# Second pointwise layer and guides as seven block products in 28 of 32 blocks of a fused attention and perception kernel

## The chip, the cores and the metric

The kernel runs on one core of a Trainium2 chip. The metric is device time of one execution in microseconds (us), as a median over runs. The engines are TensorE (PE; its weight loads are shown as PEld), VectorE (DVE), ScalarE (ACT), GpSimd (POOL) and SyncE (SP, which issues most DMAs). Each engine works through its own instructions in the order in which the program issued them. Everything is float32.

## The reference

Two layers over images of 4 x 64 x 64 pixels with 256 channels:

```python
# layer 0: global attention, per image, over its 4096 pixels
q = x @ Wq + bq;  k = x @ Wk + bk            # 32 channels each
v = x @ Wv + bv                              # 256 channels
x = gamma * (softmax(q @ k.T) @ v) + x
# layer 1: perception and 3x3 local attention
perceived = depthwise_conv3x3(x, w_perc) + b_perc        # 256 -> 768 channels
hid = gelu(w_up1 @ perceived + b_up1)                    # 768 -> 512
h   = x + w_up2 @ hid + b_up2                            # 512 -> 256, "second pointwise layer"
q, k, v = split(w_qkv @ h + b_qkv)                       # 256 each
out = h + sum over the 3x3 neighbours n of softmax_n(q . k[n] / 16) * v[n]
```

## The kernel before

**Slots.** The work is cut into 32 slots (`NSLOT`), one for each block of 512 query pixels (8 image rows); 8 slots make an image. In slot `s` PE computes the global attention of block `s`, while the later stages of earlier blocks run beside it: the depthwise convolution (`perceive`) of block `s - 2`, then for block `k = s - 3` the first pointwise layer (`hidden_part`), the second (`update`), guides (`guide`), the scores and the values of the local attention, and for block `a = s - 5` the local attention's output (`local_product`).

**Points.** A slot has 16 points, one for each 256 keys. The order is written out by hand: at each point the program issues, in this order, the energies and exponentials of a later point, the *jobs* of the point (the list `jobs`, L943), the attention's product (eight matmuls in the trace, L313), DVE's softmax add `add_up` (L327), and a share of the convolution's steps (taps on DVE, L468, and sums of quarters, L474; 60 steps over 14 points). Every engine receives its instructions in this order, so a DVE instruction of a job stands behind the taps of the point before.

**Block products.** A pointwise layer is a matrix product. `hidden_part` already writes it by blocks: the weight and the values are cut 2 x 2, and seven products of blocks with half the rows and half the columns take the place of eight, at the price of sums and differences of blocks. The differences of weights (`wmix`, from `mix_weights`, on POOL) are made once; those of values are made for each block on DVE (L474, then L539 on the results).

**The second layer and guides, before.** `update(s, c)` (L584) multiplies for each of two channel halves four weight blocks of 128 x 128 by 512 pixels of `hid` into one PSUM bank. DVE adds the bias and `x` and writes `h` in two column halves (L595). After the second half `border_terms` (L714) puts the image edge's terms into `edge` (DVE, L718 and L719). `guide(s, i)` (L667) does the same with `wg`, the product of the local query and key weights, and ACT writes the result with its bias into `guides` (tile `lq`, L681). In the job list the updates stand at points 6 and 7, point 8 has no job, and guides stand at 9 and 10, before the scores at 11 and 12.

**PSUM.** Jobs take their banks in turn from two (`job_bank`), so a job's matmuls wait until the results of the job two before have been read.

**Last slot and tail.** Slot 31 has a job list of its own. After it, blocks 29 to 31 are finished in a written order (`run`, L1047), in which DVE's last taps (`conv`) are dealt out between the jobs. `local_total` (L857) is PE's sum for the local softmax, `border` (L730) its edge term. `local_product` (L871) multiplies by the inverse sum on DVE (L889) and adds `h`: on POOL (L899) for most blocks, on DVE for blocks 28, 29 and 31. POOL also adds everything it is shown to `watched` (`watch`, L186), whose sum decides at the end whether a slower second path has to run (it does not here).

Of the kernel before, what the change touches and what calls it, by code (L numbers as in the profile page):

```python
# [15 lines left out]
P = 128  # L16
# [36 lines left out]
def attention_then_perception_kernel(  # L53
# [34 lines left out]
    def unshifted():  # L88
# [132 lines left out]
        def project_qk(s):  # L221

            ps = bank("m", f"qk_{s}")
            for kin in range(CH):
                for r in range(2):
                    nc.tensor.matmul(  # L226
                        ps[2 * r * CQK : 2 * (r + 1) * CQK, :],
                        lhsT=wqk[:, kin].rearrange("p s d -> p (s d)"),
                        rhs=staged[s + r][:, kin, :], start=(kin == 0), stop=(kin == CH - 1),
                    )  # L230
            st = tile_of([P, NB], "st", f"st_{s}")
            nc.scalar.activation(st, ps, AF.Identity, bias=bqk2)
            if s == 0:
                queries[0] = tile_of([P, NB], "qa", "qa_0", 2)
                for j in range(GRP):
                    nc.sync.dma_start(
                        out=queries[0][j * CQK : (j + 1) * CQK, :], in_=st[:CQK, :]
                    )
            for r in range(2):
                at = 2 * r * CQK  # L240
                keys[s + r] = tile_of([P, P], "ka", f"ka_{s + r}", NBLK + 1)
                queue = nc.sync if s + r else nc.scalar
                for j in range(GRP):
                    queue.dma_start(
                        out=keys[s + r][j * CQK : (j + 1) * CQK, :],
                        in_=st[at + CQK : at + 2 * CQK, bass.ts(j, P)],
                    )
                if s + r:
                    nc.sync.dma_start(
                        out=packed[:, bass.ts(s + r, NB)], in_=st[at : at + CQK, :]  # L250
                    )

        def project_v(s, pair, tag="m"):
            xc = staged[s]
            if pair == 0:
                values[s] = tile_of([P, TPB, C], "v", f"v_{s}", NBLK + 1)
# [173 lines left out]
            return thirds.pop(0)  # L430

        def spare(name):
            return tile_of([P, TPB, C], "v", name, NBLK + 1).rearrange(
                "p (a t) c -> p a (t c)", a=2
            )

# [68 lines left out]

        wmix = pool.tile([P, 4, MULT, C], F32, tag="wmix", name="wmix")

        def mix_weights():
            y = [[wup1[:, i * MULT : (i + 1) * MULT, bass.ts(j, C)] for j in range(2)] for i in range(2)]
            for to, a, b in (  # L510
                (0, y[0][1], y[0][0]), (1, y[1][1], wmix[:, 0]), (2, y[1][1], y[0][1]),
                (3, y[1][0], wmix[:, 1]),
            ):
                nc.gpsimd.tensor_tensor(wmix[:, to], a, b, ALU.subtract)

        def hidden_part(s, d, part):

# [66 lines left out]
        def update(s, c):  # L584
# [17 lines left out]
            if c == CH - 1:  # L602
                border_terms(s)

# [8 lines left out]
        def combine_steps():  # L613

            names, ws, turned = ("wq", "wk"), [], []
            ins, outs = (
                perc_tile(f"wqk_{name}").rearrange("p s n -> p (s n)") for name in ("in", "turned")
            )
            for i, name in enumerate(names):
                w = ins[:, i * NB : (i + 1) * NB].rearrange("p (k c) -> p k c", c=C)  # L620
                nc.sync.dma_start(out=w, in_=w_qkv[:, :, i * C : (i + 1) * C])
                ws.append(w)
            yield
            for i, (name, w) in enumerate(zip(names, ws)):
# [20 lines left out]
            nc.vector.tensor_copy(wg, ps.rearrange("p (k c) -> p k c", c=C))  # L645
            yield
# [20 lines left out]
        def guide(s, i):  # L667


            if s == 0 and i == 0:  # L670
                guides.append(tile_of([P, CH, UP + RB, W], "lq", "lq"))
                nc.vector.memset(guides[0][:, :, :UP, :], 0.0)
            elif i == 0:
                nc.scalar.copy(guides[0][:, :, :UP, :], guides[0][:, :, RB:, :])
            ps = job_bank(f"g_{s}_{i}")
            for kin in range(CH):
                nc.tensor.matmul(  # L677
                    ps, lhsT=wg[:, kin, bass.ts(i, P)], rhs=pixels(s, kin),
                    start=(kin == 0), stop=(kin == CH - 1),
                )  # L680
            nc.scalar.activation(  # L681
                guides[0][:, i, UP:, :].rearrange("p h w -> p (h w)"), ps, AF.Identity,
                bias=bg[:, i : i + 1],
            )


# [184 lines left out]
        def local_product(s, c, behind=None):  # L871
# [18 lines left out]
            if s < NSLOT - 1:  # L890
                watch(o)
            engine, res = nc.gpsimd, o
            if s >= DIRECT and s != NSLOT - 2:

                if c == 0:
                    results[s] = tile_of([P, CH, NB], "xc", f"res_{s}", 2)
# [40 lines left out]
        for slot in range(NSLOT):  # L937
            b, g = divmod(slot, NBLK)
            if slot >= RING:
# [4 lines left out]
                job(hidden_part, k, 0, 0) + job(local_values, k - 1, 1),  # L944
                job(local_denominator, a) + job(hidden_part, k, 0, 1),
                job(hidden_part, k, 1, 0), job(hidden_part, k, 1, 1),
                job(local_product, a, 0), job(local_product, a, 1),
                job(update, k, 0), job(update, k, 1), [],
                job(guide, k, 0), job(guide, k, 1), job(scores, k, 0),
                job(scores, k, 1) + job(local_sum, k - 1), job(local_values, k, 0), job(border, k), [],  # L950
            ]
            if slot in (1, 2):
# [9 lines left out]
            n_mixed = NPC * (TAPS - 1) + MULT * len(MIXED)  # L962
            n_steps, stepped = n_mixed, 0
            if slot == NSLOT - 1:


                jobs = [
# [17 lines left out]
            for point in range(points):  # L985
# [27 lines left out]
                if slot == 0 and point == NG:  # L1013
# [8 lines left out]
                    mix_weights()  # L1022
# [34 lines left out]
        for _ in perceive(last - 1, lower):  # L1057
# [443 lines left out]
```

## Time and profile before

| what | before |
|---|---|
| median of 3 runs | 3495.58 us (3494.74 to 3495.85) |
| profiled execution: time | 3495.72 us |
| profiled execution: span | 3494.0 us |
| PE busy | 3473.1 us, 99% |
| DVE busy | 2493.2 us, 71% |
| ACT busy | 1084.0 us, 31% |
| POOL busy | 616.4 us, 18% |
| granted TensorE clock, mean | 0.998 |

A line of a timeline gives the start, the busy time, the engine, the source line and operation, output and inputs by name with their shapes, and how many instructions were merged; in brackets the idle time before it and who ended that. Spans of single instructions overlap where an engine pipelines them, so a step's cost is better read from one start to the next. Lines `L...` are those of the kernel before.

### The profile page before, as it was taken

The page shows a single profiled execution, that of the slowest core. Times are in us where ns is not written, and L with a number is a line of the kernel's source. Part 1 is how long each engine was busy: PE and PEld are TensorE (multiplying, and loading weights), DVE is VectorE, ACT ScalarE, POOL GpSimd, SP SyncE. Part 2 cuts the span into 40 slices and gives each one's busy share as a digit, 9 for nine tenths or more (in the row PEclk, how much of TensorE's full clock was granted, in tenths as well). Part 3 has the DMA queues.
Part 4 walks back from the last instruction along what each step waited for, and adds up shares of the span by engine and source line. Part 5 has one row for each costly group of instructions (what it writes and reads, how often), then busy time and mean ns, then how long its engine had stood idle before and what let it go on. Part 6 is the DMA issues. An engine that isn't in the chain of part 4 may idle for free.

```text
span 3494.0 us, 32246 instructions
## 1 busy us (share of the span) xinstructions
PE 3473.1 (99%) x12222; PEld 1907.4 (55%) x12222; DVE 2493.2 (71%) x3631; ACT 1084.0 (31%) x1330; POOL 616.4 (18%) x823
## 2 busy tenths in 40 slices
PE   9999999999999999999999999999999999999997
PEld 5444555555555555565555555556555555555655
DVE  2387777657777877765777777776577777777885
ACT  3233332333233233332332323333333323223331
POOL 2000112111121211121112212111121121121224
PEclk9999999999999999999999999999999999999999
DMA  4000000120000000011000000001100000000000
GB/s 105 7 4 10 7 16 11 27 48 22 9 12 11 16 16 16 22 25 46 16 16 16 3 13 16 16 22 37 34 16 16 16 9 10 13 16 16 7 6 26
DMA packets 92995, 66.82 MB, mean 19 GB/s; under 512 B 65856, under 2 KB 70976, under 8 KB 92704
## 3 DMA queue, kind: packets, MB, share of 16 engines
q1 hardware_dynamic: 92160, 64.29, 6.9%
q8 instruction: 98, 1.61, 0.2%
q14 instruction: 65, 0.53, 0.0%
q10 hardware_dynamic: 672, 0.39, 0.0%
HBM read 43.49 MB, written 18.81 MB: 18 GB/s over the span
## 4 chain that ended last, share of the span: by engine, by line
PE 98%; DVE 1%; POOL 1%; SPq 0%; DMA 0%; ACT 0%; issue 0%; ACTq 0%; POOLq 0%
PE acc L313 51%; PE e L294 8%; PE dx L589 6%; PE hid_de L532 4%; PE hid_gf L532 4%; PE hid_bc L532 4%; PE g L677 3%; PE lv L746 3%; PE v L260 3%; PE lo L877 3%; PE hid_a L532 3%; PE s L787 2%; PE hid L564 1%; PE qk L226 1%; DVE perc L468 0%; POOL watched L186 0%
## 5 line engine op out<-in xcount | busy, mean ns | idle before, releaser
L313 PE MATMUL acc<-p,v 128*128 128x512 f32 x4096 | 1841.5, 594 | 0.2 <-DVE o L378 0.2
L313 PEld LDWEIGHTS acc<-p,v 128*128 128x128 f32 x4096 | 765.9, 190 | 863.4 <-issue 854.4
L468 DVE SCALAR_TENSOR_TENSOR perc<-xp,wperc,perc 128x512 f32<-128x512 f32 (+2 forms) x1554 | 1157.6, 804 | 31.8 <-ACT perc L464 31.8
L302 ACT ACTIVATE p<-e 128x1024 f32<-128x1024 f32 x512 | 524.3, 1024 | 1673.9 <-PE e L294 617.7
L327 DVE TENSOR_TENSOR den<-den,p 128x1024 f32<-128x1024 f32 x480 | 586.0, 1221 | 99.2 <-ACT p L302 97.5
L186 POOL TENSOR_TENSOR watched<-watched,lo 128x256 f32<-128x256 f32 x124 | 150.8, 1216 | 1013.5 <-DVE lo L889 1008.5
L294 PE MATMUL e<-qa,ka 32*128 32x512 f32 x2048 | 291.9, 640 | 0.0
L811 POOL TENSOR_TENSOR lp<-lp,near 128x396 f32<-128x396 f32 x60 | 87.1, 1452 | 1123.8 <-ACT lp L807 1123.8
L589 PE MATMUL dx<-hid,wup 128*128 128x512 f32 x512 | 233.0, 598 | 0.0
L759 DVE TENSOR_TENSOR lv<-lv,blv 128x256 f32<-128x256 f32 x126 | 47.5, 419 | 210.4 <-PE lv L746 210.2
L474 DVE TENSOR_TENSOR perc<-perc 128x256 f32<-128x256 f32 x360 | 173.2, 495 | 7.2
L294 PEld LDWEIGHTS e<-qa,ka 32*128 32x128 f32 x2048 | 80.0, 182 | 166.2 <-issue 164.2
L589 PEld LDWEIGHTS dx<-hid,wup 128*128 128x128 f32 x512 | 94.6, 190 | 129.9 <-issue 101.7
L532 PE MATMUL hid_de<-perc,wmix 128*128 128x256 f32 x720 | 165.2, 379 | 0.0
L532 PEld LDWEIGHTS hid_de<-perc,wmix 128*128 128x128 f32 x720 | 136.8, 190 | 43.7 <-issue 21.5
L555 ACT ACTIVATE hid<-hid,bup 128x512 f32<-128x512 f32 x120 | 80.1, 715 | 214.3 <-DVE hid L539 214.3
L539 DVE TENSOR_TENSOR hid<-hid_bc,hid 128x512 f32<-128x512 f32 x60 | 41.5, 691 | 147.3 <-PE hid_bc L532 147.3
L464 ACT ACTIVATE perc<-xp,bperc,wperc 128x512 f32<-128x512 f32 x192 | 145.1, 805 | 0.0
L595 DVE SCALAR_TENSOR_TENSOR h<-dx,bup,xp 128x256 f32<-128x256 f32 x128 | 56.0, 479 | 116.2 <-PE dx L589 116.2
L677 PE MATMUL g<-h,wg 128*128 128x512 f32 x256 | 123.4, 605 | 0.2
L746 PE MATMUL lv<-wlv,h 128*128 128x256 f32 x520 | 122.4, 379 | 0.0
L877 PEld LDWEIGHTS lo<-lp,lv 128*128 128x128 f32 x732 | 102.9, 191 | 35.1 <-issue 27.0
(147 smaller groups left out, 2898.7 us busy)
## 6 DMA issues: line engine op xcount, KB each, us to landing
xp<-in_x SPq DMA_DIRECT2D x30, 528.0 KB, 4.0
out<-lo SPq DMA_DIRECT2D x58, 256.0 KB, 2.0
xc<-in_x SPq DMA_DIRECT2D x56, 256.0 KB, 3.8
qa<-packed SPq DMA_DIRECT2D x124, 64.0 KB, 2.1
ka<-st SPq DMA_DIRECT2D x124, 16.0 KB, 1.8
packed<-st SPq DMA_DIRECT2D x31, 64.0 KB, 1.9
wup<-in_w_up SPq DMA_DIRECT2D x1, 1536.0 KB, 6.9
out<-res SPq DMA_DIRECT2D x6, 256.0 KB, 2.2
```

The costliest lines, as they stand in the source:

```text
L186: nc.gpsimd.tensor_tensor(at, at, values[:, i : min(n, i + C)], ALU.add)
L294: nc.tensor.matmul(e[:, j, :], lhsT=key[rows, :], rhs=queries[s][rows, :], start=True, stop=True,)
L302: nc.scalar.activation(p, energies[s, G][:, 2 * half : 2 * half + 2, :], AF.Exp)
L313: nc.tensor.matmul(accs[s][c], lhsT=v[:, 2 * half + i, bass.ts(c, P)], rhs=p[:, i, :], start=(first and i == 0), stop=(G == NG - 1 and hal ...
L327: nc.vector.tensor_tensor(den, den, p, ALU.add)
L468: nc.vector.scalar_tensor_tensor(acc, win, wt, acc, ALU.mult, ALU.add)
L474: nc.vector.tensor_tensor(t[:, to, :], t[:, a, :], t[:, b, :], op)
L532: nc.tensor.matmul(ps[:, n * C : (n + 1) * C], lhsT=w(j), rhs=mixes[s, j][:, kind, :], start=(j == 0), stop=(j == MULT - 1),)
L589: nc.tensor.matmul(ps, lhsT=wup2[:, d, bass.ts(c, P)], rhs=hids[s][:, d, :], start=(d == 0), stop=(d == NHC - 1),)
L677: nc.tensor.matmul(ps, lhsT=wg[:, kin, bass.ts(i, P)], rhs=pixels(s, kin), start=(kin == 0), stop=(kin == CH - 1),)
L746: nc.tensor.matmul(ps[:, half * C : (half + 1) * C], lhsT=keys_of(s, t, half, kin), rhs=wlv[:, kin, :], start=(kin == 0), stop=(kin == CH ...
L877: nc.tensor.matmul(pv[:, rows, columns(half)], lhsT=lvs[block, t, half][:, bass.ts(c, P)], rhs=near_ws[block, half][:, t, of, :], start=(i ...
```

## The change

The second pointwise layer and guides of blocks 0 to 27 are written as seven block products each. `update_mix` and `guide_mix` make the sums and differences of the value blocks on DVE; `update_part` and `guide_part` do the products in four parts (`ab`, `cd`, `eg`, `f`), and `gather` adds the results on DVE, after one copy by ACT. Weight mixes (`wmix2`, `gmix`) are made on POOL before slot 3, one of them in place in `wup2`; that half of `wup2` is loaded again in slot 31, where blocks 28 to 31 use the old form. To make room, the tiles `v` and `ka` have eight buffers in place of nine. In the tail, `local_total` of block 29 and `border` of block 30 stand before the last taps' end in place of behind the first matmuls of the last block, and block 30's residual is added on DVE in place of POOL.

```diff
-        def mix_weights():
-            ...
+        def mix_weights(y11, y12, y21, y22, t1, t2, t3, t4):
+            for to, a, b in ((t1, y12, y11), (t2, y22, t1), (t3, y22, y12), (t4, y21, t2)):
+                nc.gpsimd.tensor_tensor(to, a, b, ALU.subtract)
...
+        def seven(name, kin, *todo):
+            ps = job_bank(name)
+            for n, (w, values) in enumerate(todo):
+                for j in range(kin):
+                    nc.tensor.matmul(
+                        ps[:, n * C : (n + 1) * C], lhsT=w(j), rhs=values(j),
+                        start=(j == 0), stop=(j == kin - 1),
+                    )
+            return [ps[:, n * C : (n + 1) * C] for n in range(len(todo))]
+
+        def gather(part, ps, q11, q12, q21, q22, biases):
+            ...
+            if part == "ab":
+                a, b = ps
+                nc.scalar.copy(q22, a)
+                add(q11, b, q22, 0)
+            elif part == "cd":
+                c, d = ps
+                add(q22, c, q22)
+                add(q21, d, q22)
+            elif part == "eg":
+                e, g = ps
+                add(q12, e, q22)
+                add(q22, e, q21, 1)
+                add(q21, g, q21, 0)
+            else:
+                add(q12, ps[0], q12, 1)
...
+        def update_mix(s):
+            ...
+            nc.vector.tensor_tensor(mix1, b12, b22, ALU.add)
+            nc.vector.tensor_tensor(b12, b11, b12, ALU.subtract)
+
+        def update_part(s, part):
+            if part == "ab":
+                below(s)
+            ...
+            todo = dict(
+                ab=((y11, v11), (y21, v21)), cd=((t2, v11), (y12, v12)),
+                eg=((t1, v1), (t4, v22)), f=((y22, v21),),
+            )[part]
+            ps = seven(f"dx_{s}_{part}", CH, *todo)
+            if part == "ab":
+                nc.vector.tensor_tensor(b11, mix1, b11, ALU.subtract)
+                nc.vector.tensor_tensor(b21, b21, b11, ALU.subtract)
+            gather(...)
+            if part == "f":
+                for c in range(CH):
+                    for half in range(2):
+                        ...
+                        nc.vector.scalar_tensor_tensor(
+                            h, h, bup2[:, c : c + 1],
+                            xv[:, c, ring(s) : ring(s) + RB, at : at + KW], ALU.add, ALU.add,
+                        )
+                guide_mix(s)
+                border_terms(s)
...
+        def guide_mix(s):
+            ...
+            for to, a, b, op in (
+                (t[0], b12, b22, ALU.add), (t[2], b11, b12, ALU.subtract),
+                (t[1], t[0], b11, ALU.subtract), (t[3], b21, t[1], ALU.subtract),
+            ):
+                nc.vector.tensor_tensor(to, a, b, op)
+
+        def guide_part(s, part):
+            if part == "ab":
+                guide_above(s)
+            ...
+            todo = dict(
+                ab=((y11, b11), (y21, b21)), cd=((t2, m2), (t3, m3)),
+                eg=((t1, m1), (t4, b22)), f=((y22, m4),),
+            )[part]
+            gather(part, seven(f"g_{s}_{part}", 1, *todo), ...)
...
-            if s >= DIRECT and s != NSLOT - 2:
+            if s >= DIRECT:
...
-                job(local_product, a, 0), job(local_product, a, 1),
-                job(update, k, 0), job(update, k, 1), [],
-                job(guide, k, 0), job(guide, k, 1), job(scores, k, 0),
+                job(local_product, a, 0), job(local_product, a, 1) + job(update_mix, k),
+                job(update_part, k, "ab"), job(update_part, k, "cd") + job(update_part, k, "eg"),
+                job(update_part, k, "f"), job(guide_part, k, "ab") + job(guide_part, k, "cd"),
+                job(guide_part, k, "eg") + job(guide_part, k, "f"), job(scores, k, 0),
...
             if slot == NSLOT - 1:
+                nc.sync.dma_start(out=wup2[:, :CH, P:], in_=w_up2[:, :CH, P:])
...
-            (scores, last - 1, 0, 2), (scores, last - 1, 1, 2),
+            (scores, last - 1, 0, 2), (scores, last - 1, 1, 2), (local_total, last - 2, 0),
+            (border, last - 1, 0),
         )
         for _ in conv:
             pass
         next(finishing)
         run(
-            (hidden, last, 0, 0), (local_total, last - 2, 0), (border, last - 1, 0),
-            (local_reciprocal, last - 3, 0), (hidden, last, 1, 0),
+            (hidden, last, 0, 0), (local_reciprocal, last - 3, 0), (hidden, last, 1, 0),
```

More of the change, by code (lines that the diff above doesn't have):

```diff
@@ L240, in project_qk @@
                 at = 2 * r * CQK
-                keys[s + r] = tile_of([P, P], "ka", f"ka_{s + r}", NBLK + 1)
+                keys[s + r] = tile_of([P, P], "ka", f"ka_{s + r}", NBLK)
                 queue = nc.sync if s + r else nc.scalar
@@ L255, in project_v @@
             if pair == 0:
-                values[s] = tile_of([P, TPB, C], "v", f"v_{s}", NBLK + 1)
+                values[s] = tile_of([P, TPB, C], "v", f"v_{s}", NBLK)
             ps = bank(tag, f"v_{s}_{pair}")
@@ L432, in spare @@
         def spare(name):
-            return tile_of([P, TPB, C], "v", name, NBLK + 1).rearrange(
+            return tile_of([P, TPB, C], "v", name, NBLK).rearrange(
                 "p (a t) c -> p a (t c)", a=2
@@ L506, in unshifted, with blocks_of, add @@
         wmix = pool.tile([P, 4, MULT, C], F32, tag="wmix", name="wmix")
-        def mix_weights():
[L509 to L514, printed above, removed]
+        wmix2 = pool.tile([P, 3, CH, P], F32, tag="wmix2", name="wmix2")
+        gmix = pool.tile([P, 4, P], F32, tag="gmix", name="gmix")
+        def mix_weights(y11, y12, y21, y22, t1, t2, t3, t4):
+            for to, a, b in ((t1, y12, y11), (t2, y22, t1), (t3, y22, y12), (t4, y21, t2)):
+                nc.gpsimd.tensor_tensor(to, a, b, ALU.subtract)
+        def blocks_of(w, kin, n):
+            return [w[:, i * kin : (i + 1) * kin, bass.ts(j, n)] for i in range(2) for j in range(2)]
+        def seven(name, kin, *todo):
[8 more added lines that the diff above has]
+        def gather(part, ps, q11, q12, q21, q22, biases):
+            def add(to, a, b, out=None):
+                bias = biases[out] if biases and out is not None else None
+                if bias is None:
+                    nc.vector.tensor_tensor(to, a, b, ALU.add)
+                else:
+                    nc.vector.scalar_tensor_tensor(to, a, bias, b, ALU.add, ALU.add)
+            if part == "ab":
[11 more added lines that the diff above has]
+                add(q21, g, q21, 0)
+            else:
+                add(q12, ps[0], q12, 1)
         def hidden_part(s, d, part):
@@ L603, in update, with quarter, by_rows @@
                 border_terms(s)
+        def quarter(s, c, n):
+            return pixels(s, c)[:, n * KR : (n + 1) * KR]
+        def by_rows(t):
+            return t.rearrange("p (h a w) -> p h a w", a=2, w=KW)
+        update_mixes = {}
+        def update_mix(s):
+            q = hids[s].rearrange("p d (a n) -> p (d a) n", a=2)
+            b11, b12, b21, b22 = (q[:, i : i + 3 : 2, :] for i in (0, 1, 4, 5))
+            mix1 = tile_of([P, NB], "lsum", f"hmix_{s}").rearrange("p (d n) -> p d n", d=2)
+            update_mixes[s] = b11, b12, b21, b22, mix1
+            nc.vector.tensor_tensor(mix1, b12, b22, ALU.add)
[3 more added lines that the diff above has]
+                below(s)
+            b11, b12, b21, b22, mix1 = update_mixes[s]
+            y11, y12, y21, y22 = (lambda j, y=y: y[:, j] for y in blocks_of(wup2, CH, P))
+            t1, t2, t4 = (lambda j, i=i: wmix2[:, i, j] for i in range(3))
+            v11, v12, v21, v22, v1 = (lambda j, b=b: b[:, j] for b in (b11, b12, b21, b22, mix1))
+            todo = dict(
[6 more added lines that the diff above has]
+                nc.vector.tensor_tensor(b21, b21, b11, ALU.subtract)
+            gather(
+                part, [by_rows(t) for t in ps],
+                *(quarter(s, c, n) for n in range(2) for c in range(2)), None,
+            )
+            if part == "f":
+                for c in range(CH):
+                    for half in range(2):
+                        h = hs[s][:, c, half, HALO:, :]
+                        at = 1 + half * KW
+                        nc.vector.scalar_tensor_tensor(
+                            h, h, bup2[:, c : c + 1],
+                            xv[:, c, ring(s) : ring(s) + RB, at : at + KW], ALU.add, ALU.add,
+                        )
+                guide_mix(s)
+                border_terms(s)
         guides, lvs, near_ws, late, results, totals = [], {}, {}, {}, {}, {}
@@ L645, in combine_steps @@
             nc.vector.tensor_copy(wg, ps.rearrange("p (k c) -> p k c", c=C))
+            mix_weights(
+                *(w[:, 0] for w in blocks_of(wg, 1, P)), *(gmix[:, i] for i in range(4))
+            )
             yield
@@ L665, in combine_steps, with guide_above, guide @@
             yield
-        def guide(s, i):
-            if s == 0 and i == 0:
+        def guide_above(s):
+            if s == 0:
                 guides.append(tile_of([P, CH, UP + RB, W], "lq", "lq"))
                 nc.vector.memset(guides[0][:, :, :UP, :], 0.0)
-            elif i == 0:
+            else:
                 nc.scalar.copy(guides[0][:, :, :UP, :], guides[0][:, :, RB:, :])
+        def guide(s, i):
+            if i == 0:
+                guide_above(s)
             ps = job_bank(f"g_{s}_{i}")
@@ L683, in guide @@
                 bias=bg[:, i : i + 1],
+            )
+        guide_mixes = {}
+        def guide_mix(s):
+            b11, b12, b21, b22 = (quarter(s, c, n) for c in range(2) for n in range(2))
+            t = [
+                by_rows(o[:, i * C : (i + 1) * C])
+                for o in (tile_of([P, NB], "o", f"gmix_{s}_{i}", 2) for i in range(2))
+                for i in range(2)
+            ]
+            guide_mixes[s] = t
+            for to, a, b, op in (
[5 more added lines that the diff above has]
+            if part == "ab":
+                guide_above(s)
+            b11, b12, b21, b22 = (
+                lambda j, c=c, n=n: quarter(s, c, n) for c in range(2) for n in range(2)
+            )
+            m1, m2, m3, m4 = (lambda j, t=t: t for t in guide_mixes[s])
+            y11, y12, y21, y22 = (lambda j, y=y: y[:, 0] for y in blocks_of(wg, 1, P))
+            t1, t2, t3, t4 = (lambda j, i=i: gmix[:, i] for i in range(4))
+            todo = dict(
+                ab=((y11, b11), (y21, b21)), cd=((t2, m2), (t3, m3)),
+                eg=((t1, m1), (t4, b22)), f=((y22, m4),),
+            )[part]
+            gather(
+                part, seven(f"g_{s}_{part}", 1, *todo),
+                *(
+                    guides[0][:, i, UP + n * KR : UP + (n + 1) * KR, :].rearrange("p h w -> p (h w)")
+                    for n in range(2) for i in range(2)
+                ),
+                [bg[:, i : i + 1] for i in range(2)],
             )
@@ L1021, in unshifted @@
                     wup2 = loaded(w_up2, "wup2")
-                    mix_weights()
+                    mix_weights(
+                        *blocks_of(wup1, MULT, C), *(wmix[:, i] for i in range(4))
+                    )
+                    y = blocks_of(wup2, CH, P)
+                    mix_weights(*y, wmix2[:, 0], wmix2[:, 1], y[1], wmix2[:, 2])
                     bup2 = loaded(b_up2, "bup2")
```

## The prediction

> **What bounds the kernel now.** I read the page's busy times and its chain first, then the window table over slots (one slot is one 512-token query block), then the timeline of one slot on DVE and on PE, then the tail.
>
> ```profile
> PE 3473.1 (99%) x12222; PEld 1907.4 (55%) x12222; DVE 2493.2 (71%) x3631; ACT 1084.0 (31%) x1330; POOL 616.4 (18%) x823
> ...
> PE 98%; DVE 1%; POOL 1%; SPq 0%; DMA 0%; ACT 0%; issue 0%; ACTq 0%; POOLq 0%
> ```
>
> ```profile
> 2070.80:2174.00 103.20, 103.20 (x362) 56.17 (x361) 77.89 (x114) 32.27 (x39) 18.70 (x26) 1.00 0.04 13
> 2380.20:2518.50 138.30, 138.30 (x522) 82.43 (x521) 78.55 (x114) 44.40 (x59) 18.07 (x24) 1.00 0.20 44
> ```
>
> The chain is PE, and in a slot (columns: length, busy PE, PEld, DVE, ACT, POOL, clock) PE is busy for all of it. So a PE microsecond saved is a microsecond of time, as long as PE finds its operands ready. DVE has 25 us of slack per slot, but that is an average. The timeline of slot 21 (from 2070.8) shows where the slack lies:
>
> ```profile
> 2108.11 0.68 DVE L889 TENSOR_TENSOR lo<-lo,lrden 128x512 f32<-128x512 f32 x1
> 2108.71 1.21 DVE L327 TENSOR_TENSOR den<-den,p 128x1024 f32<-128x1024 f32 x1
> 2109.84 4.68 DVE L468 SCALAR_TENSOR_TENSOR perc<-xp,wperc,perc 128x512 f32<-128x512 f32 x4
> 2115.37 0.88 DVE L595 SCALAR_TENSOR_TENSOR h<-dx,bup,xp 128x256 f32<-128x256 f32 x2 [0.86 <-PE dx L589]
> ...
> 2122.24 0.88 DVE L595 SCALAR_TENSOR_TENSOR h<-dx,bup,xp 128x256 f32<-128x256 f32 x2 [2.21 <-PE dx L589]
> ...
> 2124.97 3.40 DVE L468 SCALAR_TENSOR_TENSOR perc<-xp,wperc,perc 128x512 f32<-128x512 f32 x5
> 2128.28 1.22 DVE L327 TENSOR_TENSOR den<-den,p 128x1024 f32<-128x1024 f32 x1
> ...
> 2133.57 2.12 DVE L468 SCALAR_TENSOR_TENSOR perc<-xp,wperc,perc 128x512 f32<-128x512 f32 x3 [0.69 <-ACT perc L464]
> ```
>
> ```profile
> 2111.63 3.70 PE L589 MATMUL dx<-hid,wup 128*128 128x512 f32 x8
> 2115.17 3.60 PE L313 MATMUL acc<-p,v 128*128 128x512 f32 x8
> ...
> 2130.17 1.88 PE L677 MATMUL g<-h,wg 128*128 128x512 f32 x4
> ...
> 2141.74 1.50 PE L787 MATMUL s<-lq,h 128*128 128x198 f32 x8
> ```
>
> From the two local products (`lo`) to the scores (`s`) at 2141.74, DVE idles only 0.86 + 2.21 + 0.69 = 3.8 us. The change puts its DVE work in just this stretch.
>
> **PE part.** Each written matmul appears as two passes. From start to start a 512-column pass takes 0.429 us (eight from 2115.17 to 2118.60) and a 256-column one 0.2145 us (six `hid_bc` passes take 1.29). The update goes from 16 passes of 512 (6.86 us) to 28 of 256 (6.01). Guides go from 8 of 512 (3.43) to 14 of 256 (3.00). That is **1.29 us less per block, 36 us in 28 blocks**, if nothing waits. The 0.19 us weight load still fits under a 0.2145 us pass, as it does in `hid_bc`.
>
> **DVE part.** What counts is the pitch, start to start: duration minus 0.08, or plus 0.04 where an instruction needs the result of the one just before it. From the rows: softmax add (L327) 1.134; tap (L468) 0.663; 512-wide add (L329, 0.692) 0.61 or 0.73; 256-wide add (L759, L474, 0.42) 0.34 or 0.46; 256-wide three-operand add (L595, 0.476) 0.40 or 0.52. Now I add up slot 21 as changed, in us after 2100, in DVE's program order.
> - Point 5 ends at 14.44 (last tap's end 14.52 minus 0.08). `update_mix`'s two 512-wide adds come in front: +1.34, 15.78. POOL's three instructions there stretch the taps (4.68 for four instead of 2.73). They are the same three, so I take that loss as unchanged.
> - Point 6: two 512-wide subtractions and one add 1.68, softmax add 1.13, four taps 2.65: 21.25. PE's `cd` needs the first subtraction, done at 16.47; PE gets there at 16.78 (11.63 + 1.72 + 3.43). No wait.
> - Point 7: five adds from `cd`, `eg` 2.06, softmax add 1.13, five taps 3.32: 27.76.
> - Point 8: `f` add 0.34, four residual adds (the last must end before its reader) 1.71: 29.81. PE, unhindered, wants `h` for guide `ab` at 29.10 (`cd`, `eg` to 20.21, product 23.64, energy 24.81, `f` 25.67, product 29.10). **PE waits 0.8** with start-up. `guide_mix` 1.48: 31.29; its third result (30.91) holds PE's guide `cd` another 0.15. Border terms 0.81, softmax add, tap and three mixes 3.06 (as 2128.28 to 2131.34): 35.16.
> - Point 9: `ab` and `cd` adds 1.32, softmax add 1.13, one mix, three taps 2.33: 39.94.
> - Point 10: `eg`, `f` adds, the last to its end, 1.85: 41.79.
>
> The scores' second channel half needs that last add. Wake-up is 0.05, and the first pass after a wait is 0.10 longer (in the tail: residual add ends 3459.28, guide matmul 3459.33, first pass 0.697 against 0.592): 41.94. It began at 41.74 + 2 x 0.167 = 42.07 before. The sum ends 0.13 us ahead; some new instructions wait for two engines, with an extra 0.02 us entry each, so I take **0.1 us per plain slot, not 1.29**. DVE, with no idle left from 2102 to 2142, sets the pace. After it, DVE needs about 12.7 us for points 10 to 12, 2 us more for POOL, 8 us to the partial sums (2153.68 to 2161.83): done near 2164.5, and PE asks at 2166.1. No second wait, but little room.
>
> **By kind of slot.** Blocks 0 to 27 run in slots 3 to 30.
> - 17 plain: -0.1 each, -1.7.
> - 6 at image edges (10, 11, 18, 19, 26, 27) have four border instructions more, 0.87 us, now in the stretch: +0.75 each, +4.5.
> - 3 projection slots (7, 15, 23): the 138 us row gives DVE 60 us of slack, spread over the points: full -1.29, -3.9.
> - 2 slots without local products (3, 4): DVE is 5 us shorter, PE 3: -2.6.
>
> Sum -3.7.
>
> **Tail.**
>
> ```profile
> 3424.26 1.22 PE L564 MATMUL hid<-perc,wup 128*128 128x512 f32 x1 [5.64 <-DVE perc L468]
> ```
>
> ```profile
> 3480.90 1.54 POOL L899 TENSOR_TENSOR lo<-lo,h 128x512 f32<-128x512 f32 x1
> ...
> 3484.33 1.26 POOL L899 TENSOR_TENSOR lo<-lo,h 128x512 f32<-128x512 f32 x1
> ```
>
> PE idles 5.64 us for the last taps, and its next four passes take 3.36 us in place of 1.72. `local_total` and `border`, 1.9 us, move into that idle time, which also breaks it up: PE can start them at 3415.1 and the mask they need ends at 3419.28. Next hidden block at 3426.3 in place of 3429.5: -3.2 (only -1.9 if the slow passes stay). POOL's two residual adds (2.8 us) stand in the chain that ends last. On DVE they fit before 3479.8, and the next late thing is DVE's residual add to 3483.67: -2.1 of the 2.8. **Tail -5.3.**
>
> **At nothing.** Nine to eight `v` and `ka` buffers: a reused buffer's last reader is a matmul just ahead in PE's own order; cover gone, a copy of 0.59 us would wait. `spare` tiles follow the same rule. `guide_mix` writes into buffers that the local results left: POOL and the output DMA (issued at 2113.33, 2.0 us) are done 14 us before. The update's mix borrows the local sum's tile, which POOL wants back 20 us later. POOL's weight mixes before slot 3: POOL is idle there, its queue holds only range checks; each is under 1.85 us (L514 at 768 columns). Reload of half of `wup2` in slot 31: 128 KB on SP, needed four points (over 25 us) later, while 1536 KB landed in 6.9 us; behind it wait only query loads of later points. ACT loses two 0.69 us activations and gains two 0.37 us copies, beside PE.
>
> **Total.** -3.7 - 5.3 = -9.0. The profiled execution took 3495.72 (span 3494.0, 1.7 around it), the median is 3495.58: **3487 us.** About 0.2% (7 us) can be told from no change.
>
> **Bounds.** New adds write runs of 32: nearest rows 0.42 (L759, contiguous) and 0.48 (L595, runs of 32, one operand more). I took 0.42, because L595 pays 0.05 for its third operand as L468 does against L329; at 0.48, ten adds cost +0.6 a slot, +14 us. POOL against `update_mix`: 0 taken, +1.0 (a tap beside L899 took 1.75, not 0.74), +23. Below: PE can save no more than 1.29 a slot, which is 3454.
>
> [...]
>
> **Rivals.**
> - *DVE lag dominates (slower).* Place: points 6 to 10. Price: 23 us for each us by which the stretch is longer than summed. It decides from +0.4 us a slot (9.0 / 23); at +1.0 the time is 3510. For it: no idle left, and each bound above points this way. Chance 0.27.
> - *DVE keeps up.* If held instructions cost no more than unheld ones (13 times 0.12), the stretch is over 1 us shorter and most of 1.29 comes: 3460 to 3475. For it: the same scheme in `hidden_part` shows PE at 100%. Against: there DVE idles 4 us before. Chance 0.25.
> - *Clock.* The 5.64 us gap halved the pass rate for 3.4 us (+1.64). If gaps of 0.8 did so, +38: 3525. Against: gaps here are seven times shorter. Chance 0.03.
>
> The forecast's own band, 3480 to 3494, has 0.45. Faster than 3488.6: 0.25 and over half of the band, 0.51. Slower than 3502.6: 0.18. Between: 0.31. Range 3464 to 3510.
>
> **What would show it.** PE busy near 3437 and DVE near 2790 (10.6 us more in each of 28 blocks). Waits of PE's guide `ab` for `h` (about 0.8), for `guide_mix` (0.15) and of scores for `lq` (0.35), in 23 slots and in none of the projection slots. Plain slots at 103.0, edge slots near 103.9, projection slots at 136.9. Plain slots at 102 or at 104 would prove the DVE sum wrong.

## The result, and the profile after

The changed kernel takes **3489.56 us** (median of 4 runs, 3488.93 to 3489.69) against 3495.49 us for the kernel before beside it (4 runs, 3494.74 to 3495.85). The ratio is 0.9983, with a 95% interval of 0.9966 to 1.0: its upper end is no change, though the two sets of runs do not overlap. That is 5.9 us less, where 9.0 were forecast. The profiled execution has a span of 3487.6 us against 3494.0.

Busy times of the page (line numbers in this and the later rows are those of the kernel profiled):

```profile
PE 3454.0 (99%) x12726; PEld 1995.1 (57%) x12726; DVE 2796.8 (80%) x4249; ACT 1063.4 (30%) x1328; POOL 694.3 (20%) x829
```

DVE has 304 us more work, close to the 297 of the forecast. PE shows 19 us less instead of 36, a first sign that PE waits for operands. The window table, one slot of each kind (plain, projection, which also projects the next image, and edge), says where (length, busy PE, PEld, DVE, ACT, POOL, clock). A slot is counted here from one start of the softmax sum's copy to the next:

```profile
2069.53:2172.62 103.09, 102.51 (x380) 59.25 (x379) 88.69 (x135) 31.64 (x39) 21.72 (x26) 1.00 0.04 14
2378.83:2515.83 137.00, 137.00 (x540) 85.81 (x539) 88.13 (x136) 43.74 (x59) 19.34 (x24) 1.00 0.20 45
2722.04:2826.01 103.97, 102.69 (x380) 59.17 (x379) 89.96 (x139) 31.68 (x39) 22.31 (x24) 1.00 0.04 13
```

The plain slot (first row) was 103.13 by this count and is 103.09. It kept its length although 1.29 us of matrix passes left it. The projection slot fell from 138.23 to 137.00 and PE is busy for all of it. The edge slot rose from 103.14 to 103.97. (The prediction says "slot 21" for the slot from 2070.8. Counted from 0, as its list of edge and projection slots is, that one is slot 20. Nothing in the sum hangs on the name.)

What PE waits for in the slots, from the waits (total us, times, longest):

```profile
PE g_cd L525 <- DVE gmix L798: 13.4, 23, 0.7
...
PE s L924 <- DVE lq L539: 5.0, 8, 0.7
```

Both releasers are DVE. In the plain slot DVE has no gap above 0.11 us over the whole stretch (2103.7 to 2140.6); the rows that matter:

```profile
2107.40 0.68 DVE L660 TENSOR_TENSOR hmix<-hid 128x512 f32<-128x512 f32 x1
2108.11 1.10 DVE L661 TENSOR_TENSOR hid<-hid 128x512 f32<-128x512 f32 x1
2109.13 1.74 DVE L327 TENSOR_TENSOR den<-den,p 128x1024 f32<-128x1024 f32 x1
2110.80 3.74 DVE L468 SCALAR_TENSOR_TENSOR perc<-xp,wperc,perc 128x512 f32<-128x512 f32 x4
...
2126.45 0.42 DVE L537 TENSOR_TENSOR h<-dx_f,h 128x256 f32<-128x256 f32 x1
2126.79 1.67 DVE L689 SCALAR_TENSOR_TENSOR h<-h,bup,xp 128x256 f32<-128x256 f32 x4
2128.55 0.76 DVE L798 TENSOR_TENSOR gmix<-h 128x256 f32<-128x256 f32 x2
2129.22 0.42 DVE L798 TENSOR_TENSOR gmix<-gmix,h 128x256 f32<-128x256 f32 x1
...
2140.09 0.48 DVE L539 SCALAR_TENSOR_TENSOR lq<-g_f,small,lq 128x256 f32<-128x256 f32 x1
```

```profile
2128.05 1.16 PE L525 MATMUL g_ab<-h,wg 128*128 128x256 f32 x4
2129.79 1.10 PE L525 MATMUL g_cd<-gmix,gmix 128*128 128x256 f32 x4 [0.58 <-DVE gmix L798]
...
2140.23 1.66 PE L924 MATMUL s<-lq,h 128*128 128x198 f32 x8
```

The rows on the two engines fit together: the mixed operand of guide part `cd` ends on DVE at 2129.64, and PE starts that part at 2129.79. The last guide add begins at 2140.09, ends at 2140.57, and the scores, begun at 2140.23, are stretched across it (1.66 us where eight passes took 1.50 before).

### The profile page after: what moved, and what is told of

Same layout as the page of the kernel before. It is cut to its first block, busy times and chain, and to the rows that moved or that the text cites. A ratio compares the mean times of both kernels' runs of the same rounds, so it can differ in the third digit from the quotient of the medians.

```text
span 3487.6 us, 34030 instructions
## 1 busy us (share of the span) xinstructions
PE 3454.0 (99%) x12726; PEld 1995.1 (57%) x12726; DVE 2796.8 (80%) x4249; ACT 1063.4 (30%) x1328; POOL 694.3 (20%) x829
## 3 DMA queue, kind: packets, MB, share of 16 engines
q8 instruction: 102, 1.67, 0.2%
## 5 line engine op out<-in xcount | busy, mean ns | idle before, releaser
L327 DVE TENSOR_TENSOR den<-den,p 128x1024 f32<-128x1024 f32 x480 | 604.6, 1259 | 85.4 <-ACT p L302 83.6
L186 POOL TENSOR_TENSOR watched<-watched,lo 128x256 f32<-128x256 f32 x124 | 136.8, 1103 | 1015.8 <-DVE lo L1026 1010.7
L948 POOL TENSOR_TENSOR lp<-lp,near 128x396 f32<-128x396 f32 x60 | 77.5, 1291 | 1137.9 <-ACT lp L944 1132.9
L969 POOL TENSOR_TENSOR lsum<-lsum,lp 128x99 f32<-128x99 f32 x168 | 132.0, 792 | 11.0
L186 POOL TENSOR_TENSOR watched<-watched,o 128x256 f32<-128x256 f32 x128 | 109.6, 856 | 43.2 <-DVE o L378 35.7
L260 PE MATMUL v<-wv,xc 128*128 128x256 f32 x512 | 116.3, 380 | 0.1
L883 PEld LDWEIGHTS lv<-wlv,h 128*128 128x128 f32 x520 | 98.7, 190 | 27.5 <-issue 15.5
```

The source lines that it names most:

```text
L186: nc.gpsimd.tensor_tensor(at, at, values[:, i : min(n, i + C)], ALU.add)
L260: nc.tensor.matmul(ps[:, i * C : (i + 1) * C], lhsT=xc[:, kin, bass.ts(2 * pair + i, P)], rhs=wv[:, kin, :], start=(kin == 0), stop=(kin = ...
L327: nc.vector.tensor_tensor(den, den, p, ALU.add)
L883: nc.tensor.matmul(ps[:, half * C : (half + 1) * C], lhsT=keys_of(s, t, half, kin), rhs=wlv[:, kin, :], start=(kin == 0), stop=(kin == CH ...
L969: nc.gpsimd.tensor_tensor(to, to, near_ws[block, half][:, t_, of, :], ALU.add)
```

## The experiments

The theory: in a plain slot PE could finish in 101.9 us, and DVE's program order from the local products to the scores sets the pace, by some 1.2 us. The main rival: PE's shorter passes are not as cheap as summed, or waits on PE cost start-up time, and DVE's order does not matter. Slot lengths are in us, in the count used above, and come from the one profiled execution of each kernel.

| kernel | median us | ratio [95%] | plain | edge | projection |
|---|---|---|---|---|---|
| before | 3495.49 | 1 | 103.13 | 103.14 | 138.23 |
| after | 3489.56 | 0.9983 [0.9966, 1.0] | 103.10 | 103.97 | 137.00 |
| border terms twice | 3517.13 | 1.0062 [1.0045, 1.0079] | 103.90 | 105.65 | 137.48 |
| border terms late | 3479.64 | 0.9956 [0.994, 0.9973] | 102.86 | 103.0 to 103.2 | 137.00 |
| mix early | 3461.93 | 0.9904 [0.9887, 0.992] | 101.90 | 102.65 | 137.00 |
| both | **3455.59** | 0.9887 [0.987, 0.9903] | 101.90 | 101.90 | 137.00 |
| update alone | 3468.24 | 0.9922 [0.9905, 0.9938] | 102.31 | 102.31 | 137.41 |
| guides alone | 3478.52 | 0.9951 [0.9935, 0.9968] | 102.72 | 102.72 | 137.82 |
| no watch on local results | 3460.00 | 0.9898 [0.9882, 0.9915] | 101.90 | 102.47 | 137.00 |
| both, no watch | 3456.75 | 0.989 [0.9873, 0.9906] | 101.90 | 101.90 | 137.00 |

**Border terms twice: is DVE the pace?** 0.81 us of DVE work is put a second time at its place (1.68 at edges); PE's work is untouched.

```
@@ update_part, part "f"
                 border_terms(s)
+                border_terms(s)
```

> The border terms are computed twice in each of the 28 blocks: 0.81 us more DVE work in the stretch between the local products and the scores (1.68 in the edge blocks), nothing on PE. If DVE's work in that stretch sets a slot's length, each plain slot gets 0.8 us longer (103.9), each edge slot 1.7 (105.6), projection slots stay at 137.0: +24 us, 3513. If the saving was lost on PE itself (short matmuls that cost more than half of a long one), a DVE at 80% has room for this: 3490.

Plain slots grew by 0.80 and edge slots by 1.68: one us of DVE is one us of time. The rival is out. The total came 4 us above what the DVE theory gave, because projection slots (+0.48), slot 3 (+1.7) and slot 31 with the tail (+1.1) grew too, which I had not counted. The last of these is not border work: the tail's code is the same, and a stretch of lowered clock (0.50 from 3502.34 to 3505.75) lies at another place of it. The waits name where the added time ends:

```profile
PE s L925 <- DVE lq L539: 16.9, 25, 0.7
PE g_cd L525 <- DVE gmix L799: 13.3, 23, 0.6
PE g_eg L525 <- DVE lq L539: 10.8, 7, 1.6
```

The wait of `g_cd` is as before, since the added work stands behind its mix. The score wait now comes in 25 slots.

**Take DVE work out of the stretch, in two places.** Border terms go behind the guides' last add (late), or `update_mix` goes ahead of the first local product, where DVE waits for PE (early).

```
@@ late: update_part, part "f", and the jobs
-                border_terms(s)
-                job(scores, k, 1) + job(local_sum, k - 1), ...
+                job(border_terms, k) + job(scores, k, 1) + job(local_sum, k - 1), ...
@@ early: the jobs
-                job(local_product, a, 0), job(local_product, a, 1) + job(update_mix, k),
+                job(update_mix, k) + job(local_product, a, 0), job(local_product, a, 1),
```

> The border terms stand at point 12, behind the last result that the scores wait for. DVE theory: DVE reaches the scores' last operand 0.81 us earlier (1.68 in edge slots), but the wait of guide part cd for guide_mix (0.58 us) lies ahead of the border terms and stays, and PE then reaches the scores at the time at which they start now. So plain slots gain only some 0.3 us (102.8), edge slots 1.15 (102.8): 3477. PE theory: no change, 3490.

> The update's two mixes stand at point 4 ahead of the first local product, where DVE idles 1.58 us; they take 1.34. DVE theory: everything behind them is 1.34 us earlier, so the wait for guide_mix (0.58) and that of the scores (0.3) go: plain slots 101.85, edge slots 102.65 (their 0.87 us of border terms still reach the scores late), 3460. PE theory: 3490.

> Mixes early and border terms late together. DVE theory: PE finds everything ready, all 28 slots gain the whole 1.24 to 1.29 us of the shorter matmuls: plain and edge slots 101.85, 3455. PE theory: 3490.

Border terms late: 102.86, so only the score wait went, and the 13.4 us of `g_cd` waits stayed (the border terms stand behind the mix that they wait for). At the edges, 103.0 to 103.2 is up to 0.4 more than I expected. Mix early: 101.90, and 102.65 at the edges. Its `g_cd` waits are gone from the list, and the first line for the slots is

```profile
PE s L924 <- DVE lq L539: 3.1, 7, 0.5
```

With both, plain and edge slots alike are 101.90, and no guide or score wait on DVE is left. The window and its DVE rows show why the early mix costs nothing:

```profile
2049.18:2151.08 101.90, 101.90 (x380) 59.68 (x379) 89.18 (x136) 31.64 (x39) 21.70 (x26) 1.00 0.04 14
```

```profile
2078.97 0.69 DVE L660 TENSOR_TENSOR hmix<-hid 128x512 f32<-128x512 f32 x1
2079.69 0.69 DVE L661 TENSOR_TENSOR hid<-hid 128x512 f32<-128x512 f32 x1
2080.63 0.69 DVE L1025 TENSOR_TENSOR lo<-lo,lrden 128x512 f32<-128x512 f32 x1 [0.25 <-PE lo L1013]
```

The two mixes fill time in which DVE waits for the first local product. In the changed kernel that wait is 1.57 us; 0.25 us of it is left.

```profile
2100.98 0.69 DVE L1026 TENSOR_TENSOR lo<-lo,lrden 128x512 f32<-128x512 f32 x1 [1.57 <-PE lo L1014]
```

**This kernel is 3455.59 us (3455.18 to 3456.57), 39.3 us under the kernel before in the same comparison.** It is faster than the kernel before and the changed one: the matrix saving of the change is real, and the place of two steps in the order lost it.

**One half of the change at a time.** The update in seven products with guides in eight, and the reverse; the tail is the changed one in both.

```
@@ update alone: update_part, and the jobs
-                guide_mix(s)
-                job(update_part, k, "f"), job(guide_part, k, "ab") + job(guide_part, k, "cd"),
-                job(guide_part, k, "eg") + job(guide_part, k, "f"), job(scores, k, 0),
+                job(update_part, k, "f"), job(guide, k, 0), job(guide, k, 1), job(scores, k, 0),
@@ guides alone: the jobs (and no update_mix, no mixes of wup2, no reload)
-                job(local_product, a, 0), job(local_product, a, 1) + job(update_mix, k),
-                job(update_part, k, "ab"), ...
+                job(local_product, a, 0), job(local_product, a, 1),
+                job(update, k, 0), job(update, k, 1) + job(guide_mix, k), [],
```

> The second layer in seven products, guides in the old form. PE saves 0.86 us per block. DVE loses 4 guide mixes and 7 guide adds from the stretch (about 4.6 us). DVE theory: nothing waits, all 28 slots 0.86 shorter than before (102.27), with the tail's 5.3: 3466. PE theory (short matmuls bring nothing): 3490.

> Guides in seven products, the second layer in the old form, so guide_mix stands at point 7. PE saves 0.43 us per block. DVE theory: the 3.8 us that DVE idles in the stretch take up most of its 4.6 us more, the scores' operand is ready some 1.5 us ahead: all 28 slots 0.43 shorter (102.7), with the tail's 5.3: 3478. PE theory: 3490. If both halves alone gain and together do not, the loss is a sum that exceeds one engine's room.

Update alone saves 0.82 of its 0.86 us per slot, guides alone 0.41 of their 0.43. Neither list of waits has a guide or a score wait on DVE left. So each half by itself is worth nearly all of its passes, and what does not fit is the DVE work of both in one stretch. The changed kernel is slower than either half.

**POOL's part in it.** The stretch opens with DVE and POOL side by side. POOL's rows in the changed kernel, beside the DVE rows of 2107 to 2115 shown above:

```profile
2107.56 2.23 POOL L186 TENSOR_TENSOR watched<-watched,lo 128x256 f32<-128x256 f32 x2 [1.90 <-DVE lo L1026]
2109.87 2.13 POOL L1036 TENSOR_TENSOR lo<-lo,h 128x512 f32<-128x512 f32 x1
```

Here the local results of blocks 0 to 27 are left out of the range watch, four POOL additions per slot.

```
@@ local_product
-            if s < NSLOT - 1:
+            if DIRECT <= s < NSLOT - 1:
                 watch(o)
```

> Leaves out the range check of the local attention's results of blocks 0 to 27 (four POOL adds per slot at points 4 and 5). [...] If that belongs to the stretch's length, DVE is about 1.9 us earlier at the scores: plain and edge slots 101.9 to 102.0, 3457. If POOL's share is hidden in DVE's slack: 3490.

Plain slots reach 101.90 with the changed order untouched; only edges (102.47) stay above. The total is 3460.0, 3 us above what I wrote; those edges are among it, and a tail 1.9 us longer than the changed kernel's (250.22 against 248.34); 1.6 us of that is there already at the last block's second hidden half, behind 6.8 us at a clock of 0.50 (see the tail in the next section). The DVE rows of the same place in a plain slot, to be set beside those of the changed kernel above:

```profile
2088.64 0.68 DVE L660 TENSOR_TENSOR hmix<-hid 128x512 f32<-128x512 f32 x1
2089.36 1.64 DVE L661 TENSOR_TENSOR hid<-hid 128x512 f32<-128x512 f32 x1
2090.92 1.21 DVE L327 TENSOR_TENSOR den<-den,p 128x1024 f32<-128x1024 f32 x1
2092.06 2.73 DVE L468 SCALAR_TENSOR_TENSOR perc<-xp,wperc,perc 128x512 f32<-128x512 f32 x4
```

```profile
2088.80 1.65 POOL L1036 TENSOR_TENSOR lo<-lo,h 128x512 f32<-128x512 f32 x1 [2.81 <-DVE lo L1026]
```

The softmax add takes 1.21 in place of 1.74 and the four taps 2.73 in place of 3.74; the second mix, now with POOL's remaining residual add (from 2088.80) beside it, takes 1.64 in place of 1.10. The net in these rows is 1.0 us, where 1.9 was expected (four taps before: 4.68 - 2.73).

The reordered kernel without the watch asks whether anything is left beyond PE (edits of both kernels above together):

> Mixes early, border terms late, and the range check of the local results of blocks 0 to 27 left out. Without that check the changed kernel came to 3460. If PE is the only limit left once mixes and border terms stand right, nothing is to be had from freeing DVE and POOL further: 3455.6, slots at 101.9. If DVE still held PE somewhere: below 3455.

It took 3456.75 (3454.89 to 3456.96), no less than with the watch. With DVE out of the way PE alone sets the slots (101.90 in both kernels).

**The tail in parts.** The slots keep the changed form. First the whole tail as before (its list and POOL's residual adds), then only the residual adds of the last-but-one slot on POOL, then only the two steps `local_total` and `border` behind the first half of the hidden layer.

```
@@ residual on POOL
-            if s >= DIRECT:
+            if s >= DIRECT and s != NSLOT - 2:
@@ order of the tail
-            (scores, last - 1, 0, 2), (scores, last - 1, 1, 2), (local_total, last - 2, 0),
-            (border, last - 1, 0),
+            (scores, last - 1, 0, 2), (scores, last - 1, 1, 2),
...
-            (hidden, last, 0, 0), (local_reciprocal, last - 3, 0), (hidden, last, 1, 0),
+            (hidden, last, 0, 0), (local_total, last - 2, 0), (border, last - 1, 0),
+            (local_reciprocal, last - 3, 0), (hidden, last, 1, 0),
```

> The changed kernel with the tail as before. If the tail gave 5.3 us as summed: 3494.8, with the 5.6 us wait of the last block's first matmuls back and POOL's two residual adds back in the chain that ends last. If the gain of 5.9 came from the slots: 3490.

> The changed kernel, but block 30's residual is added on POOL again; the new order of the tail stays. By the summed term (2.1 us) 3491.7. In the two traces the sum over watched starts 4.5 us earlier, counted from the start of slot 31, of which 2.6 were there already at the last block's second hidden matmuls: so 1.9 to 2.7 us, 3491.5 to 3492.3. If POOL's adds were covered, 3489.6.

> The changed kernel, but local_total and border stand behind the last block's first hidden matmuls again; the residual stays on DVE. By the summed term (3.2 us, the slow passes gone) 3492.8; by the two traces, where five hidden passes after the broken-up wait are still slow, 2.6 us: 3492.2.

- Old tail: 3494.89 (10 runs, 3493.73 to 3495.31), ratio 0.9998 [0.9989, 1.0008]. Without the tail's part, the change is worth nothing that can be told from zero.
- Residual on POOL: 3491.43 (10 runs, 3490.98 to 3493.04), ratio 0.999 [0.9981, 1.0]: 1.9 us above the changed kernel, as summed from the rows.
- Old order: 3494.46 (10 runs, 3493.58 to 3494.97), ratio 0.9998 [0.9988, 1.0007]: 4.9 us above the changed kernel. I had expected 3492.2 to 3492.8, a miss by some 2 us. The two parts are 1.9 and 4.9 one at a time, and 5.3 together.

The windows of 10 us just behind the 5.64 us wait of PE hold a large part of the reason; first the kernel before, then the old order (the clock is the third number from the end):

```profile
3424.00:3434.00 10.00, 9.74 (x31) 5.45 (x32) 3.36 (x6) 3.52 (x4) 2.27 (x4) 0.83 0.00 0
```

```profile
3422.00:3432.00 10.00, 9.44 (x27) 5.89 (x28) 3.66 (x6) 3.10 (x4) 2.53 (x4) 0.66 0.00 0
```

The same wait, for the same producer, was followed by a granted clock of 0.83 in one kernel and 0.66 in the other. Cut finer, the clock is 0.50 for one stretch of 3.4 us in the kernel before and for two such stretches in the old order:

```profile
3423.98:3427.39 3.41, 3.13 (x4) 1.46 (x5) 3.24 (x6) 0.00 (x0) 1.86 (x2) 0.50 0.00 0
```

```profile
3421.90:3425.31 3.41, 2.75 (x4) 1.15 (x5) 3.24 (x6) 0.00 (x0) 2.16 (x3) 0.50 0.00 0
3425.31:3428.72 3.41, 3.41 (x12) 2.89 (x11) 0.52 (x1) 0.69 (x1) 0.00 (x0) 0.50 0.00 0
```

The last block's second hidden half then begins 190.6 us behind the start of slot 31 in the old order, and 189.1 in the kernel before: 1.5 us, most of the miss, as far as one profiled execution of each can say. So the price of this wait is not a constant; what sets it, no run says.

## Why the prediction was right, and where it was wrong

**Right in direction, and two thirds of the size; the total owes something to luck.** The tail is worth 5.25 us between the two traces, as forecast; of the 5.93 us between the medians that leaves some 0.7 for everything ahead of it, where 3.7 were forecast (the old-tail kernel says 0.5). Between the traces slot 31 starts 1.1 us earlier, but 0.8 of that lies ahead of slot 2, where no changed step runs. So the slots gave almost nothing where 3.7 us were forecast. Step by step:

- *PE, 36 us less if nothing waits:* shown. Update alone gives 0.82 of 0.86 and guides alone 0.41 of 0.43 a slot; with the order mended the slots give 1.23 of 1.29.
- *DVE's order sets the pace, not PE:* shown by the doubled border terms (1.0 us of time per us of work) and by both moved steps. The point-by-point sum put the end of the add of `f` at 70.95 us behind the slot's start; measured, 71.04.
- *Plain slots -0.1 each, -1.7 in all:* measured -0.03, and slots 6 and 12 lengthened by 0.1 and 0.3, so the 17 came to about -0.1 in all. In slot 12 DVE idled 0.46 us ahead of a guide add; why, no run says. This term failed by 1.6 us, the largest error in the slots.
- *Edge slots +0.75, projection slots -1.29:* +0.84 and -1.24.
- *Slots 3 and 4, -2.6 together:* -0.36 and -1.24. In slot 3 the sum left out work: block 0 has eight border instructions and two clearing instructions (MEMSET) on DVE, and its scores waited 0.6 us. The cover of "DVE is 5 us shorter" was an average again.
- *Which PE instruction waits:* wrong. I had guide `ab` waiting 0.8 us for `h`, `cd` 0.15 for its mix and the scores 0.35. No `ab` wait exists: its first product reads one channel half only, whose residual adds end first, and it began at 2128.05 while the last residual add ended at 2128.46. The wait stands at `cd`, 0.58 us in 23 slots, and the scores' wait is a gap of its own in 8 only; in the plain slot shown it is a longer pass. The time per slot did not change by that, because DVE's order fixes when the scores may end. PE busy near 3437 failed for a like reason: passes that wait for an operand in mid-group are recorded as longer passes (`g_ab` 1.16 us, with both steps moved 1.03). With both steps moved the page gives PE 3438.4.
- *Stretch by POOL taken as unchanged:* shown. Before, four taps paid 4.68 - 2.73 = 1.95 us; after, the second mix 0.41, the softmax add 0.53 and the taps 1.01, together 1.95. The bound of +23 us fell with it.
- *DVE's pitch, duration minus 0.08, or plus 0.04 for an instruction that needs the result just before it (the "held" one of the rivals):* shown in the new rows. The four residual adds of L689 take 1.67 us where one of the same form takes 0.48, a start every 0.40; the second mix (2108.11) starts 0.03 us behind the end of the first (2107.40 + 0.68).
- *Tail -5.3:* the total is right (slot 31 with the tail 253.58 before, 248.34 after), its parts are not. The hidden layer's second half began 2.6 us earlier, not 3.2; the judging of the values, behind POOL's residual adds, gained a further 1.9, not 2.1; and 0.7 after that I had not summed. That these errors cancel is luck. The step that failed is "which also breaks it up": breaking the idle time into pieces was to spare the slow passes. In this execution it did not:

```profile
3415.65 0.46 PE L994 MATMUL ld<-lv,ones 128*128 128x99 f32 x2 [1.02 <-DVE lv L948]
...
3418.21 0.46 PE L994 MATMUL ld<-lp,ones 128*128 128x99 f32 x2 [1.51 <-DVE lp L948]
```

```profile
3418.50:3428.50 10.00, 10.00 (x25) 4.59 (x25) 7.97 (x10) 2.23 (x3) 6.61 (x8) 0.83 0.00 0
```

Behind two gaps of 1.0 and 1.5 us the clock is 0.83 over 10 us, as it was behind the one gap of 5.64, and five passes in a row start 0.68 to 0.85 us apart instead of 0.43. The prediction had named the lesser value, -1.9, for this case; what came was between the two. The kernel with the update alone shows why. It has the same two gaps, and its clock stayed at 1.00:

```profile
3393.07 0.47 PE L993 MATMUL ld<-lv,ones 128*128 128x99 f32 x2 [1.02 <-DVE lv L947]
...
3395.63 0.46 PE L993 MATMUL ld<-lp,ones 128*128 128x99 f32 x2 [1.51 <-DVE lp L947]
...
3400.78 3.55 PE L605 MATMUL hid<-perc,wup 128*128 128x512 f32 x7 [0.79 <-DVE perc L468]
```

```profile
3395.92:3405.92 10.00, 9.21 (x26) 3.96 (x26) 7.96 (x10) 2.24 (x3) 6.61 (x8) 1.00 0.00 1
```

There the second half began 3.0 us earlier than in the kernel before, close to the forecast 3.2 (186.17 us behind the start of slot 31; 189.13 before, 186.54 in the changed kernel). PE then waits 0.79 us for the last taps; in the changed kernel the slow passes fill this wait, so they cost 0.4 us and not the 1.3 between the prediction's two values. Of ten profiled kernels with this order of the tail three kept the clock here (border terms twice, update alone, guides alone), five had it at 0.50 for 3.4 us and two (mix early, no watch) for 6.8; why, no run says. The three had their lowered clock nearer the end. In nine of them slot 31 and the tail have the same order of work, and took 248.3 to 250.2 us: a difference of up to 2 us between totals can come from there, and the slot lengths are the surer measure.

- *The rival "DVE lag" decides from +0.4 a slot:* the border terms doubled are that rival carried out, 27.6 us over the changed kernel for 0.8 us a plain slot and 1.7 an edge slot. *"DVE keeps up"* did not come about, yet it needed only one line in another place.

## What to carry to other kernels

An engine with 25 us of slack per slot before the change (14 after it) can still set the pace over 40 us of it: sum its program order between the last operand it needs and the first one it owes, instruction by instruction, and compare it with the other engine's arrival. When such a sum comes out within a tenth of a us of "no gain", look first for work that can go ahead of a wait or behind a debt; here moving two mixes and a few border terms was worth 34 us where the whole change was worth 6. Test the halves of a change apart, for each may be worth more alone than both together.

## What the runs showed of the hardware

- Beside POOL's additions some DVE instructions took longer and others did not. Taking four POOL additions out of a slot gave 1.2 us of time. In the rows of that place the softmax add takes 1.74 us with them and 1.21 without, four taps 3.74 and 2.73; the second mix, a 512-wide add, takes 1.10 beside the watch's additions, 1.64 beside the residual add, and 0.69 in the kernel with both steps moved. Not each pays: the first mix kept 0.68 us though a POOL addition is recorded from 0.16 us into it on (rows of 2107.40 and 2107.56). DVE's adds of a matmul's result (`lv`, L896) took 0.41 to 0.43 us in the changed kernel, in the 73 of 126 with a POOL addition recorded beside them as in the others. What decides which one pays, no run says.
- The granted clock fell to 0.50 for 3.4 or 6.8 us behind gaps of 1.0 and 1.5 us with 1.05 us of passes between them in seven kernels, and stayed at 1.00 behind the same gaps in three. It did not fall behind the gaps of 0.58 us in the slots (clock 1.00 in every slot shown). The same gap of 5.64 us left 0.83 over the next 10 us in one kernel and 0.66 in another.
- Matrix passes of 256 columns started 0.2145 us apart and those of 512 columns 0.429 in the kernel before. Of the 1.29 us per slot summed from these, 1.23 came out as time once nothing waited.
